# Centring x in its transposed layout instead of the weights, with row statistics on ScalarE and a reordered start and end

## The chip, the core and the metric

The kernel runs on one core of one Trainium2 chip. The metric is the device time of one execution in microseconds (us), median over several executions; less is better. A core has a matrix engine (PE; its weight loads are listed apart as PEld), VectorE (DVE), ScalarE (ACT), GpSimd (POOL) and SyncE (SP), which here only issues transfers. Each engine works through its own instructions strictly in order and waits on semaphores for the others. SBUF is the working memory, PSUM the memory that PE writes to.

## The reference

The input x is 4 sequences of 512 tokens with 512 features. Two blocks follow each other, each with a residual and a layer norm ahead of it:

```python
def _L0_attn_ref(x, W_q, W_kv, W_o):          # 16 heads of 32
    q  = (x @ W_q.T).reshape(B, S, H, hd)
    kv = (x @ W_kv.T).reshape(B, S, H, hd)
    qf  = _l2_normalize_complex(jnp.fft.fft(q, axis=-1))
    kvf = _l2_normalize_complex(jnp.fft.fft(kv, axis=-1))
    kvf = jnp.cumsum(kvf, axis=1)
    values_hat = jnp.fft.ifft(qf * kvf, axis=-1).real
    return values_hat.reshape(B, S, D) @ W_o.T
...
x = x + _L0_attn_ref(_layernorm(x), W_q, W_kv, W_o)
x = x + _L0_ffn_ref(_layernorm(x), gate_w, up_w, down_w, ...)   # silu(gate) * up, then down; 512 -> 1536 -> 512
```

The layer norm is (x - mean) / sqrt(var + 1e-5). The FFN's weights are rounded to float8_e4m3 first and its three products are scaled by vectors.

## The kernel before

**Setup.** The 2048 tokens are N = 16 chunks of 128 (four sequences of TC = 4 chunks). The Fourier transforms are 32x32 matrices, so they are multiplied into the weights at the start: `fold_in` turns W_kv and W_q (`raw[0]`, `raw[1]`) into `wkv` and `wq` by 16 matmuls of 128x128 each (two instructions per fp32 matmul, 32 in the profile), `fold_out` turns W_o into `wo`. A table tile `tab` holds the Fourier matrix (`fwd`, slot 0), the identity (slot 1), the inverse (slot 2) and a triangle of ones (slot 3). The transfer of slots 0 and 1 stands twice in the code (L91 and L110).

**How the mean is taken out.** q and kv are linear in x, so the mean over a token's 512 features can be removed by removing the mean over features from each row of the weights. That is `centered` (L149): for each of the four 128-row blocks of W_kv and W_q, DVE takes `bn_stats` and `bn_aggr`, then DVE (blocks 0 and 2 of W_kv) or ACT (all others, L158) subtracts. The reciprocal deviation of each token comes from `stats` (L259): `bn_stats`, `bn_aggr` and an addition of eps on DVE and a power on POOL (L266). It multiplies the spectra later.

**Rounds.** The loop over i = 0 .. 15 (L525) is a software pipeline, its order written out by hand (`tc.manual_schedule()`), so the order of the calls is the order on each engine. PE does per round `spectrum(i, 1)` (wkv, 8 matmul instructions), `v_transpose(i-2)` (four 128x128 transposes), `spectrum(i, 0)` (wq), `running(i-1)` (the cumulative sum of a chunk as a product with the triangle: `cum`) and `project(i-2)` (W_o: `po`). ACT squares the spectra (`squared`), DVE sums squares (`summed`), POOL takes the power -1/2 (`norms`, `rn`), DVE scales (`k_scaled`, `q_scaled`) and multiplies (`products`), POOL combines real and imaginary parts (`combined`). `carry` copies the last rows of a chunk's sum on ACT into `end` and sends the last one by DMA to the next chunk. `finish` adds the residual and stores the result to DRAM, `load_y` fetches it back for the FFN.

**FFN weights.** They come as 18 units of 128x1024, each rounded in four steps on DVE, ACT and POOL (`quant_abs`, `quant_step`, `quant_floor`, `quant_add`, `quant_sub`); `next_parts(n)` hands out the next n of these steps. What the rounds have not done is done inside the first FFN.

**FFN.** `ffn(b)` runs four times over m = 0 .. 11: two products `gu` (PSUM tag "b", two banks), `g` = silu on ACT (L456), `f` on DVE (L458), `fh` on ACT, `fl` on DVE, then the down product `pd`. In the last four steps m of one sequence the next one is prepared: `y_stats` (m = 8, 9), `y_norm` (m = 9, 10) and `y_transpose` (m = 10, 11; `pt_f`, `yh` on ACT, `yl` on DVE).

Work tiles come from rotating buffers: `end` and `cross` have one, most others two. PSUM has eight banks: four of tag "acc" (`pq`, `pw`, `pd`), two of "b" (`cum`, `po`, `gu`) and two of "tp" (`pt_v`, `pt_f`).

Of the kernel before, what the change touches and what calls it, by code (L numbers as in the profile page):

```python
# [30 lines left out]
def tile_fft_attention_then_fp8_ffn(  # L31
# [56 lines left out]


    tab = const.tile([P, 4, P], F32, name="tab")  # L90
    nc.sync.dma_start(tab[:, :2, :], tables[:, :2, :])  # L91
    fwd, ident, inv, tri = (tab[:, i, :] for i in range(4))

    xt, xTs = {}, {}
# [1 line left out]
    def load_xT(i):  # L96
        xTs[i] = work.tile([P, KC, P], F32, tag="xT", name=f"xT_{i}", bufs=3)
        nc.sync.dma_start(xTs[i], xT[i])

    def load_x(i):  # L100
        b, c = chunks[i]
        t = work.tile([P, D], F32, tag="x", name=f"x_{b}_{c}", bufs=6)
        nc.sync.dma_start(t, x[b, c * P : (c + 1) * P, :])
        xt[i] = t
# [2 lines left out]
        return big.tile([P, KC, D], dtype, tag="big", name=name)  # L107

    raw = []
    nc.sync.dma_start(tab[:, :2, :], tables[:, :2, :])  # L110
    for i, w in enumerate((w_kv, w_q, w_oT)):
        t = big_tile(f"raw{i}")
        for j in range(KC):
            nc.sync.dma_start(t[:, j, :], w[j * P : (j + 1) * P, :])
        raw.append(t)
        if i == 0:
            load_xT(0)
            nc.sync.dma_start(tab[:, 2:, :], tables[:, 2:, :])
        elif i == 1:
            load_x(0)  # L120
            load_xT(1)
            load_x(1)
    gus = const.tile([P, 2, MC], F32, name="gus")
    dsc = const.tile([P, D], F32, name="dsc")
    nc.scalar.dma_start(gus[:, 0, :], gate_scale)
    nc.scalar.dma_start(gus[:, 1, :], up_scale)
    nc.scalar.dma_start(dsc, down_scale.partition_broadcast(P))

    over = const.tile([P, 1], F32, name="over")
    nc.gpsimd.memset(over, -E4M3_OVERFLOW * DOWN * HUGE)  # L130

# [14 lines left out]
    wq = big_tile("wq")  # L146
    wo = big_tile("wo")

    def centered(r, j, on_act):  # L149

        t = r[:, j, :]
        st = work.tile([P, 6], F32, tag="st6", name=f"st_w{j}", bufs=3)
        nc.vector.bn_stats(st, t)
        mv = work.tile([P, 2], F32, tag="mv", name=f"mv_w{j}", bufs=8)
        nc.vector.bn_aggr(mv, st)
        if on_act:
            nc.vector.tensor_scalar(mv[:, 1:2], mv[:, 0:1], -1.0, None, ALU.mult)
            nc.scalar.activation(t, t, AF.Identity, bias=mv[:, 1:2])  # L158
        else:
            nc.vector.tensor_scalar(t, t, mv[:, 0:1], None, ALU.subtract)  # L160

    def fold_in(w, r):

        pw = [ps.tile([P, D], F32, tag="acc", name=f"pw{i}", bufs=4) for i in range(KC - 1)]
        pw.append(ps.tile([P, D], F32, tag="b", name=f"pw{KC - 1}"))
        for j in range(KC):
            for i in range(KC):
                nc.tensor.matmul(  # L168
                    pw[i][:, j * P : (j + 1) * P],
                    lhsT=r[:, j, i * P : (i + 1) * P],  # L170
                    rhs=fwd,
                    start=True,
                    stop=True,
                )
        for i in range(KC):
            (nc.scalar.copy, nc.vector.tensor_copy)[i % 2](w[:, i, :], pw[i])

    def fold_out(w, r):
        for j in range(KC):
            pw = ps.tile([P, D], F32, tag="acc", name="pw", bufs=4)  # L180
            nc.tensor.matmul(pw, lhsT=inv, rhs=r[:, j, :], start=True, stop=True)
            nc.scalar.copy(w[:, j, :], pw)


    U1 = 12
# [71 lines left out]


    def stats(src, name):  # L259
        st = work.tile([P, 6], F32, tag="st6", name=f"st_{name}", bufs=3)  # L260
        nc.vector.bn_stats(st, src)
        mv = work.tile([P, 2], F32, tag="mv", name=f"mv_{name}", bufs=8)
        nc.vector.bn_aggr(mv, st)
        rstd = work.tile([P, 1], F32, tag="rstd", name=f"rstd_{name}", bufs=8)
        nc.vector.tensor_scalar(rstd, mv[:, 1:2], EPS, None, ALU.add)  # L265
        nc.gpsimd.tensor_tensor(rstd, rstd, nhalf[:, 0:1], ALU.pow)  # L266
        return mv, rstd

    def normed(src, mv_rstd, name):
        mv, rstd = mv_rstd  # L270
        xn = work.tile([P, D], F32, tag="xn", name=f"xn_{name}")
        nc.vector.tensor_scalar(xn, src, mv[:, 0:1], rstd, ALU.subtract, ALU.mult)
        return xn

    def transpose(src, name):
# [5 lines left out]
    def heads(t):  # L281
        return t.rearrange("p (h f) -> p h f", f=HD)


    st_x, xns, pqs, sss, rns, qns, kns, carries, cums, qvs, qvTs, pos = (
        {} for _ in range(12)
    )

    def nm(i):
        return "%d_%d" % chunks[i]  # L290

    def x_stats(i):
        st_x[i] = stats(xt[i], f"a{nm(i)}")

    def spectrum(i, j):
        if j == 1:
# [9 lines left out]
    def squares(i, j):  # L306
        squared(i, j)
        summed(i, j)
# [82 lines left out]
        qvTs[i] = work.tile([P, KC, P], F32, tag="qvT", name=f"qvT_{nm(i)}")  # L391
        nc.scalar.copy(qvTs[i], pt)  # L392

    def project(i):
        po = ps.tile([P, D], F32, tag="b", name=f"po_{nm(i)}")
        qvT = qvTs.pop(i)
        for k in range(KC):
            nc.tensor.matmul(  # L398
                po, lhsT=qvT[:, k, :], rhs=wo[:, k, :], start=k == 0, stop=k == KC - 1
            )  # L400
        pos[i] = po
# [102 lines left out]
    def at(f, i, *more):  # L504
        if 0 <= i < N:
            f(i, *more)

    for j in range(KC):
        centered(raw[0], j, j % 2)
    fold_in(wkv, raw[0])  # L510
    x_stats(0)
    for j in range(KC):
        centered(raw[1], j, True)
    x_stats(1)
    nc.vector.tensor_copy(tri_r, tri)

    def attend(i):
        running(i)
        carry(i)
        products(i)  # L520
        combined(i)


    given = [4, 2, 2] + [3] * (N - 6) + [2, 2, 0]
    for i in range(N):  # L525
        at(spectrum, i, 1)
        if i == 0:
            load_unit(0)
            squares(0, 1)
            fold_in(wq, raw[1])  # L530
        if i == N - 6:
            load_y(0)
        at(load_xT, i + 2)
        if i > 2:
            k_scaled(i - 1)
        at(finish, i - 3)
        at(load_x, i + 2)
        if i > 2:
            k_low(i - 1)
        if i > 0:  # L540
            squared(i, 1)
        if i != 2:
            at(v_transpose, i - 2)
        if i > 0:
            next_parts(given[i] // 3, True)
        at(q_scaled, i - 1)
        if i > 0:
            summed(i, 1)
        at(norms, i, 1)
        if i == 0:  # L550
            fold_out(wo, raw[2])
        for c in pair(i - (N - 4)):
            y_stats(0, c)
        if i == 1:
            attend(0)
        at(spectrum, i, 0)
        if i == 0:
            quant_abs(0)
            next_parts(2, True)
        else:  # L560
            next_parts((given[i] + 1) // 3, True)
        if i == 2:
            v_transpose(0)
        if i > 1:
            running(i - 1)
        squared(i, 0)
        if i > 1:
            carry(i - 1)
        for c in pair(i - (N - 2)):
            y_transpose(0, c)  # L570
        for c in pair(i - (N - 3)):
            y_norm(0, c)
        if i > 1:
            products(i - 1)
            combined(i - 1)
        summed(i, 0)
        norms(i, 0)
        if i < 2:
            k_scaled(i)
            k_low(i)  # L580
        next_parts((given[i] + 2) // 3, True)
        at(x_stats, i + 2)
        at(project, i - 2)

# [7 lines left out]
    for b in range(B):  # L594

        def on_pe(m, part, b=b):
            if part == 0:
                if b == 0 and m < 2:
                    v_transpose(N - 2 + m)
                if b == 0 and m == 1:  # L600
                    finish(N - 2)
                return
            if b == 0 and m == 0:
                running(N - 1)
                products(N - 1)
                combined(N - 1)
                project(N - 2)
            if b + 1 < B and m >= MC - 2:
                for c in pair(m - (MC - 2)):
                    y_transpose(b + 1, c)  # L610

        def between(m, b=b):
            if b == 0 and m > 0:
                next_parts(1)

        def behind(m, b=b):
            if b == 0:
                if m == 1:
                    project(N - 1)
                    finish(N - 1)  # L620
                next_parts(2)
            if b + 1 < B:
                if m == 4:
                    load_y(b + 1)
                for c in pair(m - (MC - 3)):
                    y_norm(b + 1, c)
                for c in pair(m - (MC - 4)):
                    y_stats(b + 1, c)

        ffn(b, on_pe, between, behind)  # L630


# [60 lines left out]
```

## Time and profile before

| what | value |
|---|---|
| time, median of 3 executions | 492.27 us (490.43 to 492.43) |
| time of the profiled execution | 491.94 us |
| span of the profiled execution | 489.9 us |
| busy: PE, DVE, POOL, ACT | 470.2, 305.5, 180.2, 156.2 us |
| mean granted PE clock | 0.994 |

The span is what the profiler sees from the first to the last instruction; the time is 2.0 us more. A group's row gives busy time, the mean of one instruction in ns, and the idle time of the engine before these instructions with the engine, tile and line that ended it. The chain is followed back from the last instruction to whatever released each step. Matmuls are pipelined: the length of one is more than its distance to the next.

### The profile page before, as it was taken

To read this page: it belongs to the slowest core of one execution; us is meant where nothing else is said; L and a number is where in the kernel's file an instruction comes from. 1 tells how busy PE (TensorE), PEld (TensorE's weight loads), DVE (VectorE), ACT (ScalarE), POOL (GpSimd) and SP (SyncE) were. 2 spreads that over 40 slices of the span, in tenths; PEclk is the share of its full clock that TensorE was granted. 3 is DMA by queue.
4 is the path that set the end of the run, shared out by engine and by line. 5 is a ranking of instruction groups with operands and counts; after the bars stand their busy time and mean duration, and the time that the engine had idled before them with its cause. 6 is when DMAs were issued, how large, how long until landed. Compare 5 with 4: busy or idle time off the path is not lost.

```text
span 489.9 us, 4871 instructions
## 1 busy us (share of the span) xinstructions
PE 470.2 (96%) x1768; PEld 320.8 (65%) x1768; DVE 305.5 (62%) x499; ACT 156.2 (32%) x233; POOL 180.2 (37%) x124
## 2 busy tenths in 40 slices
PE   3999999999999999999998999999999999999995
PEld 3644444444444454568886888888888888888883
DVE  3757998889889997758788832237522246422225
ACT  2554433344433424323432322222222223222220
POOL 0226999888787975620212040001400000400002
PEclk9999999999999999999999899999999999999999
DMA  7912334115424200406000050000130000200002
GB/s 240 371 45 65 111 104 151 64 64 176 151 68 165 66 22 24 170 1 236 1 0 0 1 171 1 0 1 1 64 108 0 1 0 0 87 0 2 1 1 86
DMA packets 19080, 34.56 MB, mean 71 GB/s; under 512 B 2160, under 2 KB 2544, under 8 KB 19056
## 3 DMA queue, kind: packets, MB, share of 16 engines
q1 hardware_dynamic: 18240, 33.95, 20.3%
q10 hardware_dynamic: 816, 0.30, 0.2%
q8 instruction: 14, 0.23, 0.2%
q14 instruction: 10, 0.08, 0.1%
HBM read 25.83 MB, written 8.39 MB: 70 GB/s over the span
## 4 chain that ended last, share of the span: by engine, by line
PE 74%; DVE 16%; ACT 4%; issue 2%; POOL 1%; DMA 1%; ACTq 0%; SPq 0%; DVEq 0%
PE gu L445 34%; PE pd L483 18%; PE pq L301 11%; PE po L398 6%; PE pw L168 2%; DVE qa L237 2%; PE pt_f L278 1%; DVE ss L317 1%; DVE qm L233 1%; DVE kn L325 1%; ACT qa L226 1%; DVE qv L374 1%; DVE kl L347 1%; PE pt_v L278 1%; ACT kh L342 1%
## 5 line engine op out<-in xcount | busy, mean ns | idle before, releaser
L322 POOL TENSOR_TENSOR rn<-ss,nhalf 128x16 f32<-128x16 f32 x32 | 105.2, 3287 | 28.0 <-DVE ss L317 27.9
L458 DVE SCALAR_TENSOR_TENSOR f<-gu,gus,g 128x512 f32<-128x512 f32 x48 | 36.0, 751 | 107.2 <-PE gu L445 106.9
L483 PE MATMUL pd<-wd,fh 128*128 128x512 f32 x192 | 77.1, 401 | 0.0
L483 PE MATMUL pd<-wd,fl 128*128 128x512 f32 x192 | 76.6, 399 | 0.0
L445 PE MATMUL gu<-yh,wg 128*128 128x512 f32 x192 | 76.2, 397 | 0.4 <-DVE cross L376 0.4
L445 PE MATMUL gu<-yh,wu 128*128 128x512 f32 x192 | 74.9, 390 | 0.1
L445 PE MATMUL gu<-yl,wg 128*128 128x512 f32 x192 | 74.9, 390 | 0.0
L445 PE MATMUL gu<-yl,wu 128*128 128x512 f32 x192 | 74.8, 390 | 0.0
L456 ACT ACTIVATE g<-gu,gus 128x512 f32<-128x512 f32 x48 | 33.1, 689 | 97.4 <-PE gu L445 97.4
L463 ACT CAST fh<-f 128x512 fp32r<-128x512 f32 x48 | 29.8, 622 | 97.3 <-DVE f L458 97.3
L398 PE MATMUL po<-wo,qvT 128*128 128x512 f32 x128 | 57.7, 594 | 1.5 <-ACT qvT L392 0.8
L301 PE MATMUL pq<-wkv,xT 128*128 128x512 f32 x128 | 57.6, 593 | 0.0
L301 PE MATMUL pq<-wq,xT 128*128 128x512 f32 x128 | 57.6, 592 | 0.0
L496 POOL TENSOR_TENSOR o<-o,ys 128x512 f32<-128x512 f32 x14 | 17.7, 1293 | 90.7 <-issue 59.6
L266 POOL TENSOR_TENSOR rstd_f<-rstd_f,nhalf 128x1 f32<-128x1 f32 x16 | 8.8, 559 | 112.3 <-DVE rstd_f L265 112.3
L465 DVE TENSOR_TENSOR fl<-f,fh 128x512 fp32r<-128x512 f32 x48 | 33.2, 692 | 26.4 <-ACT fh L463 26.1
L301 PEld LDWEIGHTS pq<-wkv,xT 128*128 128x128 f32 x128 | 24.2, 190 | 30.3 <-issue 29.4
L445 PEld LDWEIGHTS gu<-yh,wg 128*128 128x128 f32 x192 | 36.2, 189 | 10.0 <-issue 1.7
L483 PEld LDWEIGHTS pd<-wd,fl 128*128 128x128 f32 x192 | 36.4, 190 | 8.6 <-DVE fl L465 0.2
L483 PEld LDWEIGHTS pd<-wd,fh 128*128 128x128 f32 x192 | 36.5, 190 | 8.2
L445 PEld LDWEIGHTS gu<-yl,wg 128*128 128x128 f32 x192 | 36.1, 188 | 8.2 <-issue 0.5
L398 PEld LDWEIGHTS po<-wo,qvT 128*128 128x128 f32 x128 | 23.9, 189 | 26.3 <-issue 23.0
(71 smaller groups left out, 584.8 us busy)
## 6 DMA issues: line engine op xcount, KB each, us to landing
xT<-in_xT SPq DMA_DIRECT2D x16, 256.0 KB, 2.8
x<-in_x SPq DMA_DIRECT2D x16, 256.0 KB, 2.8
y_all<-x SPq DMA_DIRECT2D x16, 256.0 KB, 2.0
ys<-y_all SPq DMA_DIRECT2D x4, 1024.0 KB, 5.7
out<-o SPq DMA_DIRECT2D x16, 256.0 KB, 2.0
rawf<-in_gate_w SPq DMA_DIRECT2D x3, 1024.0 KB, 5.5
rawf<-in_up_w SPq DMA_DIRECT2D x3, 1024.0 KB, 7.5
rawf<-in_down_w SPq DMA_DIRECT2D x3, 1024.0 KB, 6.1
```

The lines of the kernel that those rows point to most:

```text
L168: nc.tensor.matmul(pw[i][:, j * P : (j + 1) * P], lhsT=r[:, j, i * P : (i + 1) * P], rhs=fwd, start=True, stop=True,)
L237: nc.vector.scalar_tensor_tensor(a, m, ROUNDER / DOWN, w, ALU.mult, ALU.add)
L301: nc.tensor.matmul(pq, lhsT=xTs[i][:, k, :], rhs=w[:, k, :], start=k == 0, stop=k == KC - 1)
L322: nc.gpsimd.tensor_tensor(rns[i, j], sss.pop((i, j)), nhalf, ALU.pow)
L398: nc.tensor.matmul(po, lhsT=qvT[:, k, :], rhs=wo[:, k, :], start=k == 0, stop=k == KC - 1)
L445: nc.tensor.matmul(p, lhsT=w[:, k, m * P : (m + 1) * P], rhs=v[:, k, :], start=k == 0 and v is yh, stop=k == KC - 1 and v is yl,)
L456: nc.scalar.activation(g, pgu[0], AF.Silu, scale=gus[:, 0, m : m + 1])
L458: nc.vector.scalar_tensor_tensor(f, pgu[1], gus[:, 1, m : m + 1], g, ALU.mult, ALU.mult)
L463: nc.scalar.copy(fh, f)
L465: nc.vector.tensor_tensor(fl, f, fh.bitcast(F32), ALU.subtract)
L483: nc.tensor.matmul(pd[c], lhsT=v[:, c * P : (c + 1) * P], rhs=wd[:, n, :], start=n == 0 and v is fused[n][0], stop=n == MC - 1 and v is fu ...
L496: add.tensor_tensor(o, o, y[:, c, :], ALU.add)
```

## The change

x is centred instead of the weights. `centered` is gone. `stats` now runs on ACT: one pass sums a row (`accum_out`), a second small one makes minus the mean (`less`), a third sums the squared deviations, a fourth makes variance plus eps; POOL takes the power as before. This `stats` serves both the 16 chunks of x and the 16 of the FFN's input. Since x in its transposed layout (`xT`) has tokens along the free axis, the means are needed as a row: `x_row` spreads `less` over 128 columns and lets PE transpose it into a PSUM bank of tag "tp", and `x_center` adds that row to `xT` on DVE.

The order changes at the start, in rounds 0 and 1 (now written out), in the last three rounds, and in `behind`. Each table slot is sent once; x's first chunks are loaded earlier; the FFN's scale vectors are issued on SP's queue after the first round and no longer on ACT's at the start. `fold_in` is split into blocks, the first block of W_q going ahead of `spectrum(0, 1)`. The first two chunks of the first FFN input are transposed at the end of round N-2, its other two in round N-1; `project` of the last two chunks uses the banks of tag "tp".

```diff
-    nc.sync.dma_start(tab[:, :2, :], tables[:, :2, :])
+    nc.sync.dma_start(tab[:, 0, :], tables[:, 0, :])
...
-    nc.sync.dma_start(tab[:, :2, :], tables[:, :2, :])
     for i, w in enumerate((w_kv, w_q, w_oT)):
         t = big_tile(f"raw{i}")
         for j in range(KC):
             nc.sync.dma_start(t[:, j, :], w[j * P : (j + 1) * P, :])
+            if (i, j) == (0, 1):
+                load_x(0)
+                nc.sync.dma_start(tab[:, 1, :], tables[:, 1, :])
         raw.append(t)
         if i == 0:
             load_xT(0)
+        elif i == 1:
+            load_x(1)
+            load_xT(1)
             nc.sync.dma_start(tab[:, 2:, :], tables[:, 2:, :])
...
     def fold_out(w, r):
...
-            nc.scalar.copy(w[:, j, :], pw)
+            (nc.vector.tensor_copy, nc.scalar.copy)[j % 2](w[:, j, :], pw)
...
     def stats(src, name):
-        st = work.tile([P, 6], F32, tag="st6", name=f"st_{name}", bufs=3)
-        nc.vector.bn_stats(st, src)
-        mv = work.tile([P, 2], F32, tag="mv", name=f"mv_{name}", bufs=8)
-        nc.vector.bn_aggr(mv, st)
-        rstd = work.tile([P, 1], F32, tag="rstd", name=f"rstd_{name}", bufs=8)
-        nc.vector.tensor_scalar(rstd, mv[:, 1:2], EPS, None, ALU.add)
+        less = work.tile([P, 1], F32, tag="less", name=f"less_{name}", bufs=4)
+        rstd = work.tile([P, 1], F32, tag="dev", name=f"dev_{name}", bufs=6)
+        each = work.tile([P, D], F32, tag="end", name=f"each_{name}", bufs=1)
+        nc.scalar.activation(each, src, AF.Identity, accum_out=less)
+        nc.scalar.activation(less, less, AF.Copy, scale=-1.0 / D)
+        nc.scalar.activation(each, src, AF.Square, bias=less, accum_out=rstd)
+        nc.scalar.activation(rstd, rstd, AF.Identity, scale=1.0 / D, bias=eps)
         nc.gpsimd.tensor_tensor(rstd, rstd, nhalf[:, 0:1], ALU.pow)
...
+    def x_row(i):
+        rows[i] = ps.tile([P, KC, P], F32, tag="tp", name=f"mean_{nm(i)}")
+        nc.tensor.transpose(rows[i][:, 0, :], st_x[i][0].to_broadcast([P, P]), ident)
+
+    def x_center(i):
+        row = rows.pop(i)[:, 0:1, :].to_broadcast([P, KC, P])
+        nc.vector.tensor_tensor(xTs[i], xTs[i], row, ALU.add)
...
+    pkv = [ps.tile([P, D], F32, tag="acc", name=f"pkv{i}", bufs=4) for i in range(KC)]
     for j in range(KC):
-        centered(raw[0], j, j % 2)
-    fold_in(wkv, raw[0])
+        fold_in(pkv, raw[0], j)
     x_stats(0)
-    for j in range(KC):
-        centered(raw[1], j, True)
+    x_row(0)
+    folded(wkv, pkv)
+    x_center(0)
+    pw = ...
+    fold_in(pw, raw[1], 0)
     x_stats(1)
...
+    spectrum(0, 1)
+    squares(0, 1)
+    norms(0, 1)
+    for j in range(1, KC):
+        fold_in(pw, raw[1], j)
+    folded(wq, pw)
+    x_row(1)
+    x_center(1)
+    quant_abs(0)
+    k_scaled(0)
+    fold_out(wo, raw[2])
...
+    running(0)
+    carry(0)
+    x_stats(2)
...
+    spectrum(1, 1)
+    squares(1, 1)
+    norms(1, 1)
+    x_row(2)
+    x_center(2)
+    q_scaled(0)
+    products(0)
+    combined(0)
+    spectrum(1, 0)
...
-    for i in range(N):
+    for i in range(2, N):
...
         for c in pair(i - (N - 4)):
             y_stats(0, c)
-        if i == 1:
-            attend(0)
-        at(spectrum, i, 0)
+        spectrum(i, 0)
...
+        at(x_row, i + 1)
+        running(i - 1)
         squared(i, 0)
-        if i > 1:
-            carry(i - 1)
-        for c in pair(i - (N - 2)):
-            y_transpose(0, c)
-        for c in pair(i - (N - 3)):
-            y_norm(0, c)
+        carry(i - 1)
+        at(x_center, i + 1)
+        products(i - 1)
+        combined(i - 1)
+        if i == N - 1:
+            y_transpose(0, TC - 2)
+            y_transpose(0, TC - 1)
+        summed(i, 0)
+        norms(i, 0)
+        for c in pair(i - (N - 3)):
+            y_norm(0, c)
         next_parts((given[i] + 2) // 3, True)
         at(x_stats, i + 2)
-        at(project, i - 2)
+        project(i - 2)
+        if i == N - 2:
+            y_transpose(0, 0)
+            y_transpose(0, 1)
...
         def behind(m, b=b):
-            if b == 0:
-                if m == 1:
-                    project(N - 1)
-                    finish(N - 1)
-                next_parts(2)
+            if b == 0 and m == 1:
+                project(N - 1, "tp")
+                finish(N - 1)
             if b + 1 < B:
                 if m == 4:
                     load_y(b + 1)
                 for c in pair(m - (MC - 3)):
                     y_norm(b + 1, c)
+            if b == 0:
+                next_parts(2)
+            if b + 1 < B:
                 for c in pair(m - (MC - 4)):
                     y_stats(b + 1, c)
```

## The prediction

> **What bounds the kernel now.** First the page, for the engine that carries the span; then PE's waits, the order of time at the start, and the ends.
>
> ```profile
> span 489.9 us, 4871 instructions
> PE 470.2 (96%) x1768; PEld 320.8 (65%) x1768; DVE 305.5 (62%) x499; ACT 156.2 (32%) x233; POOL 180.2 (37%) x124
> PE 74%; DVE 16%; ACT 4%; issue 2%; POOL 1%; DMA 1%; ACTq 0%; SPq 0%; DVEq 0%
> ```
>
> PE is busy 470 of 490 us, so other engines matter only where PE waits. The view of PE's waits:
>
> ```profile
> PE pw L168 <- DVE raw L160: 7.8, 1, 7.8
> PE pt_f L278 <- DVE xn_f L272: 2.1, 1, 2.1
> PE pt_v L278 <- POOL qv L385: 1.4, 2, 1.0
> PE po L398 <- ACT qvT L392: 0.8, 1, 0.8
> PE po L398 <- DVE f L458: 0.7, 1, 0.7
> PE gu L445 <- DVE cross L376: 0.4, 1, 0.4
> ```
>
> Waits of 13.8 us in all (0.6 in smaller rows), 7.8 before the first matmul. The timeline shows what that start consists of:
>
> ```profile
> 0.72 0.37 SPq L91 DMA_DIRECT2D tab<-in_tables  x1
> 3.00 0.33 SPq L110 DMA_DIRECT2D tab<-in_tables  x1
> 3.38 2.02 SPq L114 DMA_DIRECT2D raw<-in_w_kv  x4
> 6.29 0.69 DVE L153 BATCH_NORM_STATS2 st_w<-raw 128x6 f32<-128x512 f32 x1 [6.29 <-DMA raw<-in_w_kv]
> 7.78 6.51 PE L168 MATMUL pw<-tab,raw 128*128 128x128 f32 x32 [7.78 <-DVE raw L160]
> 14.29 3.70 PE L301 MATMUL pq<-wkv,xT 128*128 128x512 f32 x8
> 17.98 4.18 PE L168 MATMUL pw<-tab,raw 128*128 128x128 f32 x32
> 22.16 3.70 PE L181 MATMUL pw<-raw,tab 128*128 128x512 f32 x8
> ```
>
> The second table transfer waits for the first, the weights stand behind it, then comes a mean. The same 32 matmuls take 6.51 us first and 4.18 us later: the early ones start 0.21 us apart, from 13.3 us on 0.11. The windows view around the one long late wait shows the clock falling there too:
>
> ```profile
> 265.90:269.30 3.40, 1.32 (x7) 0.79 (x5) 3.06 (x4) 0.29 (x1) 0.27 (x1) 1.00 0.00 0
> 269.30:272.70 3.40, 3.40 (x12) 3.03 (x13) 3.26 (x9) 0.36 (x1) 1.08 (x2) 0.51 0.00 0
> ```
>
> Columns: PE, PEld, DVE, ACT, POOL, clock, DMA. PE paused 2.1 us; in the next 3.4 us it had 0.51 of its clock. In rounds 3 to 13 PE has no gap: spectra start every 11.21 us. Between, from the groups split by shape:
>
> ```profile
> L158 ACT ACTIVATE raw<-raw,mv_w 128x512 f32<-128x512 f32 x6 | 4.3, 722 | 10.4 <-DVE mv_w L157 10.2 <-DMA rawf<-in_gate_w 0.3
> L463 ACT CAST fh<-f 128x512 fp32r<-128x512 f32 x48 | 29.8, 622 | 97.3 <-DVE f L458 97.3
> L134 ACT ACTIVATE table<-table 128x1 f32<-128x1 f32 x1 | 0.2, 202 | 0.0
> ```
>
> These price the new ACT work.
>
> **Start to fold_out.** With no second table, W_kv's first block is issued at 0.72 + 0.37 = 1.1 us. A 256 KB load takes 2.6 us at best here (shortest xT; first W_kv block 2.9), so it lands at 3.7 and PE starts at 3.75 instead of 7.78. Later blocks land 0.7 us apart and PE uses one in 1.7, so they don't hold it. The slow phase I take as the trace has it: 6.4 us from first to last, to 10.15. Rule against row: the Trainium skill (TensorE: Matmul & The Clock Gate, Part 1: The HAM clock gate) says half clock lasts until about 3.4 us of sustained work, in a window that runs freely; the trace had 5.6 us. By 3.4 us, 16 matmuls would be slow and 16 fast: 5.2 us, 1.2 better. I keep the trace; 1.2 goes into the range. The copies of wkv end 1.04 us after the last matmul (15.16 against 14.12), `x_center(0)` on DVE adds 0.69 (kl, 128x512): 11.9. PE meanwhile does the mean row and W_q's first block (1.0), and idles 0.55. Spectrum 3.69 from 11.95, the other three blocks 3.0, a row 0.15: `fold_out` starts at 18.8 instead of 22.16, -3.4. Bounds: -4.6 and -2.0 (late blocks: the third came at about 9.0, 4.5 us after its issue).
>
> **Rounds 0 and 1.** Walking the written order with the same durations: `carry(0)`'s DMA (row lands 1.8 us after issue) holds `x_stats(2)` on ACT, since `each` shares the single "end" buffer; behind it stand `qa_1` and sq1 of chunk 1; DVE waits for that sq1 ahead of `x_center(2)`; so spectrum(2,1) is 0.8 late. POOL then does rn0(0), rn1(1) (2.9 each) before qv: pt_v(0) 1.2 late. Before, the same stretch lost 1.5 us up to po(0) and 0.43 at pt_v(1). Net -0.2, between -1 and +1.5.
>
> **Mean rows.** Twelve more single transposes, chunks 4 to 15. pt_v's four take 0.435 us start to start in a stream (65.67 to 66.10), 0.11 each; with a change of operand I take 0.15: +1.8. Rule that speaks against the change: the same page (Part 4: PE-mode transpose) has about 275 ns each in a kernel, +3.3; the trace agrees with 273 ns as an instruction's length, but not as its share of PE's time. Ends +1.3 and +3.3. `x_center` (0.69) replaces 1.02 us of stats on DVE. It waits for the row, which PE makes just ahead of cum; behind it stand products, which had waited for `end` until 1 us after cum anyway, and spectrum(i+1,1) needs it 3.2 us later: nothing; uncovered it would be 0.69 a round. The row's bank, one of the two of tag "tp", is free again before the next pt_v.
>
> **Length s of one stats on ACT.** No row has an accumulating activation. Its four passes without that: 0.62 (no bias, as fh), 0.20, 0.72 (bias from a tile, as L158) and 0.30 (0.20 and the bias's 0.72 - 0.62), with three waits on the pass before of 0.04 (st_w to mv_w on DVE: 6.29 + 0.69 to 7.02): 1.96. With each accumulator read priced as the 128x1 row, 0.2, it is 2.36. I take 2.3. A gain below 1.96 is excluded: each pass must run. In the windows of rounds 11 to 13 ACT is busy 3.0 to 5.1 of 11.2 us, so one s a round is hidden. If it weren't, kh would be late first and PE would wait at `cum`.
>
> **Rounds 12 to 15.** Rounds 12 and 13 carry three s each: 6.9 + 4.8 of other work = 11.7 against 11.35. Counted from the start of round 12: ACT has kh(11), sq1(12), qvT(10) and the quant pass L226 done at 6.25, two y_stats last until 10.85, then come qa_10 (1.05) and sq0(12), done at 12.6, which a spectrum ending at 7.3 would allow at 8. DVE's ss0, quant_add and kn(12) follow at 15.2, kh(12), sq1(13) and qvT(11) at 17.1, two more y_stats until 21.7, sq0(13) and end(12) at 22.95. DVE takes products(12), ss0, two xn and the quant step behind it: 26.8; ACT's L226 waits for that step (27.95), `x_stats(15)` stands behind (30.25), kh(13) behind that (30.9), and kl ends at 31.6. PE could start cum(13) at 30.2 and is clear of it 1.6 late, waiting for qvT(12) too. Gone: pt_v's 1.0 and the 0.4 and 0.7 at the FFN's start (po no longer needs f's bank); a new 0.3 at pt_v(15). Net -0.2; ends -1.5 (s = 2.0) and +1.5 (2.55).
>
> **End of the first FFN.** Before, xn came after quant steps; now it goes first and 4.1 us of stats leave DVE. The 2.1 us go, and with them the half clock that followed: pt_f took 1.91 instead of 0.87, pd 2.62 instead of 1.87, 1.8. In exchange two y_stats at m = 8 and two at m = 9 stand ahead of g(9), g(10) on ACT. By g, f, fh, yh, yl, xn the second pt_f pair is just in time at s = 2.29; at 2.3 each of three hand-overs loses 0.05. Net -3.75, ends -3.9 and 0.
>
> **At nothing.** Scale vectors on SP: ahead of load_x(3), needed at 200 us; uncovered 0.7 us of transfers. x_0 and x_2, xT_2 are sent earlier, ahead of the first FFN weights: these landed at 21.1 (13.66 + 7.4) and now, with 128 KB more ahead and the stream 2 us sooner, at 19.4; ACT asks for them at 19.3 and has 0.5 us before kh(0) is late; uncovered, up to 1. Two wo copies on DVE beside fold_out. One quant step more in rounds, one less in FFN: DVE has room. The last o-add and store unchanged.
>
> **Sum** against the profiled 491.94: -3.4 - 0.2 + 1.8 - 0.2 - 3.75 = -5.75, so 486.2. The median of the runs, 492.27, is 0.33 above the profiled time.
>
> **Rivals.**
> 1. ACT becomes the limit, slower: if s is 2.8 (accumulator reads of 0.4). Slope: 7 us per us of s in rounds 12 to 14 (three s in each of two rounds, one after), 12 in the FFN (four s in series, three hand-overs). Against s = 2.3 that is +9.5: 495.7. Break-even near 2.6, slower by 0.5% from 2.75. For: ACT load 11.7 of 11.35 already. Against: the 0.2 row.
> 2. The start is bound by loads: W_kv and W_q blocks stretched as the third was, PE starting but waiting, stalls of rounds 0 and 1 doubled: head -0.5, sum about 489. With s = 2.45 beside it (+2.8) no change, 491.5.
> 3. The mean rows cost 0.3 to 0.4 each on PE: +2 to +3, 488.6. The change then does what it says and still gains.
> That centring x is not equivalent can be excluded: the projection is linear.
>
> **Numbers.** Forecast 0.60; rival 2 and mixtures near no change 0.20; rival 3 0.07; rival 1 0.13. What a measurement can tell from no change is about 0.5%, 2.5 us. Faster: 0.60 + 0.07 + 0.07 of rival 2 = 0.74; same 0.14; slower 0.12. Lowest: gate opening early (-1.2) and rows at 0.11 (-0.5), some bounds of rounds: 483.0. The upper end takes in the mixtures: 491.8.
>
> **What would show it.** Right: first L149 matmul near 3.8, fold_out near 19; PE waits at pt_f gone and clock 1.00 through the first FFN's end; rounds 11.36 us apart; four L247 to L250 instructions in 2.3 us. Wrong: accumulating passes over 0.9 us, PE waiting for kh or kl in rounds 13 and 14, for yl or xn at the hand-overs; first matmul after 5 us; rounds over 11.5 us.

## The result and the profile after

The changed kernel takes 487.0 us (median of 5, 486.5 to 487.3) against 492.27 (490.4 to 492.6): a ratio of 0.9905, 95% interval 0.9881 to 0.9929. The forecast was 486.2. The sum came out, but not its terms: the start and rounds 12 to 15 gained 3.1 us more than forecast, a loss of 3.6 us in the FFN was not in the forecast at all, and the two hid each other. The executions of the kernel before fall into two groups, near 490.1 and 492.1 us, and three of these five lie in the upper one; against the lower one the change gains about 3 us.

The page of the kernel after, its span, busy times and chain:

```profile
span 484.7 us, 5008 instructions
PE 471.6 (97%) x1784; PEld 318.6 (66%) x1784; DVE 281.6 (58%) x397; ACT 212.1 (44%) x417; POOL 184.4 (38%) x125
PE 82%; DMA 5%; DVE 4%; ACT 3%; POOL 3%; issue 2%; SPq 0%; ACTq 0%; DVEq 0%
```

DVE's busy time fell by 24 us and ACT's rose by 56, and DVE's share of the chain fell from 16% to 4%. PE, though it now waits less, is busy *longer* than before (470.2). PE's waits after:

```profile
PE pkv L149 <- DMA raw<-in_w_kv: 3.9, 1, 3.9
PE pt_v L263 <- POOL qv L378: 1.5, 2, 1.1
PE pw L149 <- DMA raw<-in_w_q: 0.7, 1, 0.7
PE pq L294 <- DVE xT L286: 0.4, 1, 0.4
PE cum L349 <- ACT g L449: 0.4, 1, 0.4
PE mean L282 <- ACT less L248: 0.3, 1, 0.3
PE cum L349 <- DVE kl L340: 0.2, 1, 0.2
```

They add up to 7.4 us instead of 13.8, but the span fell by 5.2 only. The start, from PE's timeline (start, length):

```profile
3.89 5.39 PE L149 MATMUL pkv<-tab,raw 128*128 128x128 f32 x32 [3.89 <-DMA raw<-in_w_kv]
10.08 1.16 PE L149 MATMUL pw<-tab,raw 128*128 128x128 f32 x8 [0.69 <-DMA raw<-in_w_q]
11.08 3.60 PE L294 MATMUL pq<-wkv,xT 128*128 128x512 f32 x8
17.30 3.88 PE L164 MATMUL pw<-raw,tab 128*128 128x512 f32 x8
```

The first matmul is 3.9 us earlier and `fold_out` 4.86 (17.30 against 22.16). At the end of the first FFN, where the kernel before paused and then lost its clock, the windows view shows PE busy throughout and the clock (last column but two) at 1.00:

```profile
257.23:263.62 6.39, 6.39 (x34) 5.25 (x32) 5.58 (x7) 5.38 (x16) 2.81 (x5) 1.00 0.01 3
263.62:270.10 6.48, 6.48 (x35) 5.34 (x34) 4.24 (x8) 2.72 (x5) 0.58 (x1) 1.00 0.00 0
```

Set against the trace before, by the starts of single matmuls:

| stretch on PE | forecast | measured |
|---|---|---|
| start to the other spectrum of round 3 (54.90 to 49.63) | -3.6 | -5.27 |
| from there to the first of round 12 (rows of chunks 4 to 12) | +1.35 | +1.60 |
| from there to the first `pd` (rows 13 to 15, rounds 12 to 15) | +0.25 | -1.20 |
| end of the first FFN | -3.75 | -3.85 |
| pace of the FFN everywhere else | 0 | +3.62 |
| to the last `pd` | -5.75 | -5.10 |

The last row but one is a term that the forecast did not have. One m of the FFN takes 5.593 us after, 5.520 before, in all four sequences, with the same 24 matmuls and no wait. The groups split by shape, over the undisturbed stretch from 290 to 470 us, before and then after:

```profile
L445 PE MATMUL gu<-yl,wu 128*128 128x512 f32 x128 | 49.9, 390 | 0.0
L445 PE MATMUL gu<-yh,wu 128*128 128x512 f32 x128 | 49.8, 389 | 0.0
L483 PE MATMUL pd<-wd,fh 128*128 128x512 f32 x129 | 51.4, 398 | 0.0
```

```profile
L438 PE MATMUL gu<-yh,wu 128*128 128x512 f32 x128 | 50.7, 396 | 0.0
L438 PE MATMUL gu<-yl,wu 128*128 128x512 f32 x128 | 50.5, 394 | 0.0
L476 PE MATMUL pd<-wd,fh 128*128 128x512 f32 x124 | 49.2, 397 | 0.0
```

Six nanoseconds an instruction: gu went from 389 to 395, to where pd was all along. From start to start, where no length is modelled, a gu followed the one before after 227.9 ns before and 233.5 ns after. That is what most of the experiments are about.

### The profile page after: what moved, and what is told of

Read it like the earlier page. It is cut to its first block, busy times and chain, and to the rows that moved or that the text cites. A ratio compares the mean times of both kernels' runs of the same rounds, so it can differ in the third digit from the quotient of the medians.

```text
span 484.7 us, 5008 instructions
## 1 busy us (share of the span) xinstructions
PE 471.6 (97%) x1784; PEld 318.6 (66%) x1784; DVE 281.6 (58%) x397; ACT 212.1 (44%) x417; POOL 184.4 (38%) x125
## 4 chain that ended last, share of the span: by engine, by line
PE 82%; DMA 5%; DVE 4%; ACT 3%; POOL 3%; issue 2%; SPq 0%; ACTq 0%; DVEq 0%
PE gu L438 36%; PE pd L476 18%; PE pq L294 15%; PE po L391 9%; POOL rn L315 2%; DMA row<-end 1%; DMA rawf<-in_gate_w 1%; DMA xT<-in_xT 1%; PE pt_v L263 1%; PE pt_f L263 1%; PE cum L349 1%; DMA raw<-in_w_kv 1%; ACT kh L335 1%; DVE kl L340 1%; ACT each L249 1%
## 5 line engine op out<-in xcount | busy, mean ns | idle before, releaser
L315 POOL TENSOR_TENSOR rn<-ss,nhalf 128x16 f32<-128x16 f32 x32 | 110.1, 3442 | 20.6 <-DVE ss L310 20.6
L438 PE MATMUL gu<-yh,wu 128*128 128x512 f32 x192 | 76.2, 397 | 0.0
L251 POOL TENSOR_TENSOR dev_f<-dev_f,nhalf 128x1 f32<-128x1 f32 x16 | 9.7, 611 | 108.4 <-ACT dev_f L250 108.3
L438 PEld LDWEIGHTS gu<-yl,wu 128*128 128x128 f32 x192 | 36.0, 188 | 8.6
L438 PEld LDWEIGHTS gu<-yh,wu 128*128 128x128 f32 x192 | 36.1, 188 | 8.6
```

The costliest lines, as they stand in the source:

```text
L315: nc.gpsimd.tensor_tensor(rns[i, j], sss.pop((i, j)), nhalf, ALU.pow)
L438: nc.tensor.matmul(p, lhsT=w[:, k, m * P : (m + 1) * P], rhs=v[:, k, :], start=k == 0 and v is yh, stop=k == KC - 1 and v is yl,)
```

## Experiments

**Where the tiles lie: three shifts of 32 bytes.** The change moved `gus` and `dsc` behind the weights and added `eps`, so yh and yl (pool "big") lie elsewhere relative to wg and wu. The first theory was that the two operands of a matmul want the same address modulo 64. All shifts use tiles that nothing reads:

```diff
+    const.tile([P, 1], F32, name="pad0")      # first run only
     wg = const.tile([P, KC, FF], F32R, name="wg")
...
     dsc = const.tile([P, D], F32, name="dsc")
+    const.tile([P, 1], F32, name="pad1")      # both runs
```

> The changed kernel with two unused 32-byte tiles, so that wg, wu, wd, yh, yl, fh and fl all start at 0 modulo 64 bytes. In the traces so far a gu or pd matmul starts 226 to 227 ns after the one before where its two operand tiles have the same address modulo 64 (gu before: 32 and 32), and about 233.6 ns (231, 232, 238 in turn) where they differ (gu after: 32 and 0; pd in both: 0 and 32). Theory, the pace follows from the two addresses: gu and pd both at 226 to 229 ns, the period of one m in the FFN 5.43 to 5.48 us instead of 5.593, total 480 to 481.5 us. Rival, the pace follows from what ACT, DVE and POOL do beside the matmuls, or differs from run to run: gu stays at 233, total 487.

> The changed kernel with one unused 32-byte tile behind dsc: the weights stay at 32 modulo 64, yh, yl, fh and fl move from 0 to 32. Theory of equal addresses: the same as with all at 0, gu and pd at 226 to 229 ns, 480 to 481.5 us. Rival, only tiles on a multiple of 64 are fast (then gu of the kernel before was fast for another reason): slower than with all at 0, gu and pd at 233 ns or more, 487 us or above. Rival, other engines set the pace: 487.

The third is the kernel before, with one such tile behind `wd`:

> The kernel before with one unused 32-byte tile behind wd: yh and yl move from 32 to 0 modulo 64, fh and fl from 0 to 32, the weights stay at 32. Theory of equal addresses: gu turns slow (226.5 to 233.6 ns) and pd turns fast (233.5 to 226.5), so the two change places; 16 matmuls gain about 5 ns each and 8 lose about 7 in one m, the period 5.52 becomes 5.54, the total rises by 1 us or less, 492 to 494. Rival, other engines set the pace: both stay as they were in the kernel before.

Measured: 485.48, 485.87 and 493.2 us. The first two gained 1.1 to 1.5 us instead of 6, so "modulo 64" fell. But the third, in which nothing but addresses moved, lost 0.35% (interval 0.18 to 0.53%), and its gu took on the pace of the changed kernel (290 to 470 us again):

```profile
L446 PE MATMUL gu<-yl,wu 128*128 128x512 f32 x125 | 49.4, 396 | 0.0
L446 PE MATMUL gu<-yh,wu 128*128 128x512 f32 x126 | 49.6, 394 | 0.0
```

In its trace one m takes 5.586 us instead of 5.520, which is 3.2 us over the 48 of them. The ratio shows less because nine of the sixteen executions of the kernel before beside it were of the upper group; the other seven have a median of 490.1. So the place of the tiles sets the pace, and the rule was wrong. What singled out gu in the kernel before was that yh and wg had equal addresses in many more low bits.

**All at multiples of 512.** Larger unused tiles in the same places, and one ahead of the work tiles:

```diff
+    work.tile([P, 112], F32, name="pad2", bufs=1)
...
+    const.tile([P, 56], F32, name="pad0")
     wg = const.tile([P, KC, FF], F32R, name="wg")
...
     dsc = const.tile([P, D], F32, name="dsc")
+    const.tile([P, 104], F32, name="pad1")
```

> The changed kernel with unused tiles so that the weights wg, wu, wd and the moving or stationary tiles yh, yl, fh, fl all start at multiples of 512 bytes. The runs with a shift of 32 bytes moved the pace but not by the rule modulo 64. Left is this: in the kernel before, wg and yh had the same address modulo 512 (352 and 352), and gu ran at 227.9 ns; in every other pairing seen (gu at a difference of 32, 96, 128; pd at 96, 128, 160, 192, all modulo 512 or 256) the mean lies between 230.8 and 234. Theory, equal addresses modulo 512 (the step from one 128-column slice of the weights to the next) are what is fast: gu and pd both 226.5 to 228 ns, the period of one m 5.43 to 5.47 us instead of 5.593, 6 to 8 us less than the changed kernel: 479 to 481 us. Rival, a property of the kernel before that has nothing to do with these differences: gu near 233, pd 231 to 233, 485 to 487 us.

480.03 us, 0.9778 of the kernel before (0.9752 to 0.9804), as the theory said. The same groups, all fast now:

```profile
L440 PE MATMUL gu<-yl,wu 128*128 128x512 f32 x131 | 51.0, 389 | 0.0
L440 PE MATMUL gu<-yh,wu 128*128 128x512 f32 x131 | 51.0, 389 | 0.0
L478 PE MATMUL pd<-wd,fh 128*128 128x512 f32 x131 | 51.3, 392 | 0.0
```

**Half of that, and the same for the kernel before.** Two more placements: yh and yl moved on by 256 bytes (`pad1` of 160 bytes, `pad2` of 704), and the kernel before with fh and fl moved so that they, too, agree with the weights.

> The changed kernel with weights, fh and fl at multiples of 512 bytes, and yh, yl at 256 modulo 512. If equality modulo 256 is enough, gu at 227 ns and the period of one m 5.44 us, 480 us; if the rule is modulo 512, gu at 231 to 234 and pd at 227, period 5.52 to 5.55, 484 to 485 us.

> The kernel before with one unused tile of 416 bytes ahead of the work tiles, so that fh and fl, like yh and yl already, have the same address as the weights modulo 512 (352). Nothing else of it is changed. Theory of equal addresses: gu stays at 227 ns, pd goes from 234 to 227, 7 ns times 8 matmuls times 48 = 2.7 us: 489.6 us where the half clock falls in, 487.7 where not. With this, both kernels have the same pace in the FFN, and what is left between this run and the changed kernel at multiples of 512 (480.0) is the change by itself: 8 to 9.5 us. Rival, the gain at multiples of 512 came from something else that the changed kernel alone has: pd stays at 234, 490.4 to 492.

480.06 us in a single execution, and 486.53 (ratio 0.9925, 0.9903 to 0.9947). The first answers its question by the pace in its trace: 256 is enough. The second missed on the size: the kernel before gained 3.9 us and not 2.7, because gu itself still had 1 ns to gain and the first gu behind pd had been slow as well (one m 5.520 to 5.440, times 48: 3.84). All placements together, with the addresses that the builds give ("operands apart" is the address of yh, yl, fh or fl minus that of its weights):

| kernel | gu: operands apart, mod 256 | gu, ns apart | pd: operands apart, mod 256 | pd, ns apart | one m, us |
|---|---|---|---|---|---|
| before | 0 | 227.9 | 96 | 234.0 | 5.520 |
| after | 96 | 233.5 | 160 | 233.2 | 5.593 |
| all at 0 mod 64 | 128 | 233.1 | 192 | 230.9 | 5.574 |
| all at 32 mod 64 | 128 | 232.9 | 192 | 230.8 | 5.573 |
| before, shifted by 32 | 32 | 232.9 | 128 | 232.4 | 5.586 |
| all at 0 mod 512 | 0 | 226.8 | 0 | 227.0 | 5.440 |
| yh, yl at 256 | 0 | 226.8 | 0 | 226.9 | 5.440 |
| before, all at 352 | 0 | 226.8 | 0 | 227.5 | 5.440 |

Every pairing at 0 runs at 227 to 228 ns, every other one tried at 231 to 234. It is the difference that counts and not a round address: the last row has all tiles at 352 modulo 512 and is as fast as all at 0. This also gives what the change is worth with the pace out of the way: 486.53 to 480.03, 6.5 us. That is less than the 8 to 9.5 expected, since the kernel before gained more by its placement than I had priced and only one of its six executions was of the upper group.

**The end of the first FFN: the order, or the move to ACT?** First the order alone, in the kernel before:

```diff
-            if b == 0:
-                if m == 1:
-                    project(N - 1)
-                    finish(N - 1)
-                next_parts(2)
+            if b == 0 and m == 1:
+                project(N - 1)
+                finish(N - 1)
             if b + 1 < B:
                 if m == 4:
                     load_y(b + 1)
                 for c in pair(m - (MC - 3)):
                     y_norm(b + 1, c)
+            if b == 0:
+                next_parts(2)
+            if b + 1 < B:
                 for c in pair(m - (MC - 4)):
                     y_stats(b + 1, c)
```

> The kernel before with only the order at the end of the first FFN changed: xn (y_norm) goes ahead of the quant steps, the statistics behind them, and stay on VectorE. Theory, the step of the forecast (the wait at pt_f of 2.1 us and the half clock behind it of 1.8 us come from the order alone): the wait goes, the clock stays at 1.00 through the end of the first FFN, 3.7 to 3.9 us less, 488.4 us. Rival, VectorE stays late because it still has 4.1 us of statistics there: a wait of about 1 us remains, half clock or not, 490 to 491.5.

489.98 us, ratio 0.997 (0.9952 to 0.9987): nearer the rival. The first pair of `pt_f` no longer waits, the second does, since DVE is still behind there. From its timeline:

```profile
271.43 0.50 PE L445 MATMUL gu<-yh,wu 128*128 128x512 f32 x1 [0.26 <-DVE f L458]
274.90 1.09 PE L278 MATMUL pt_f<-tab,xn_f 128*128 128x128 f32 x8 [1.36 <-DVE xn_f L272]
```

The clock stays up, but the m with the second pair takes 10.39 us where its like in the later sequences takes 8.26: the pause of 2.1 us has only moved by one pair. Against the seven executions of the kernel before in the lower group (median 490.1) the order alone gains nothing that is clear of noise.

Then the reverse: the changed kernel with only the statistics of y back on DVE as `bn_stats`.

> The changed kernel with the statistics of y (16 of them) back on VectorE as bn_stats, those of x left on ScalarE. Theory, the end of the first FFN needs both the order and the move (with the order alone PE still waited 1.4 us at the second pair of pt_f and 0.5 behind it): a wait of 1.4 to 2 us returns at the second pair, and at the FFN's start; rounds 12 to 14 lose less than 0.8 at cum(13), since ScalarE is freer and VectorE fuller; total 488 to 489.5. Rival, the order alone is worth it in this kernel, and statistics on ScalarE cost time in rounds 12 to 14: 486 to 486.5, faster than the changed kernel.

487.13 us, the same as the changed kernel:

```profile
270.32 1.08 PE L263 MATMUL pt_f<-tab,xn_f 128*128 128x128 f32 x8 [0.44 <-DVE xn_f L257]
```

The wait at the second pair is 0.44, not 1.4 to 2; that stretch loses 0.63 us and rounds 12 to 15 gain 0.38. So my theory fell: in the changed kernel the move of y's statistics is nearly even. What else removed the pause was not isolated. One part can be seen on DVE: in the first of these two runs it still does a quant step between the last statistics and `fl`, and in the second, with one step more done in the rounds, it has none there:

```profile
271.29 1.21 DVE L241 SCALAR_TENSOR_TENSOR wd<-qm,qa 128x1024 fp32r<-128x1024 f32 x1
```

The slower pace of PE in the changed kernel, 0.07 us for each m, also leaves DVE more time. How much each is worth stays open.

**The start.** The changed kernel with two table slots sent twice again:

```diff
-    nc.sync.dma_start(tab[:, 0, :], tables[:, 0, :])
+    nc.sync.dma_start(tab[:, :2, :], tables[:, :2, :])
...
+    nc.sync.dma_start(tab[:, :2, :], tables[:, :2, :])
     for i, w in enumerate((w_kv, w_q, w_oT)):
...
-                nc.sync.dma_start(tab[:, 1, :], tables[:, 1, :])
```

> The changed kernel with the first two tables sent twice ahead of the weights again, as in the kernel before, and nothing else of it undone. Theory of the forecast (of the 4 us by which the first matmul came earlier, the second table's wait was 2.3 and the mean of W_kv's blocks 1.5): the first matmul at 6.1 to 6.4 us instead of 3.89, fold_out and the end 2 to 2.5 us later, 489 to 489.5 us. Rival, the start is bound by later loads or by the clock gate: the first matmul moves by 2.3 us, the end by less than 1, 487.5 us.

488.77 us (1.8 more than the changed kernel), with the first matmul at 6.36:

```profile
6.36 5.30 PE L149 MATMUL pkv<-tab,raw 128*128 128x128 f32 x32 [6.36 <-DMA raw<-in_w_kv]
13.20 3.70 PE L294 MATMUL pq<-wkv,xT 128*128 128x512 f32 x8 [0.53 <-DVE xT L286]
```

2.5 us at the first matmul, 2.1 at the first spectrum, 2.2 at the last `pd`: in this trace what is lost there is not won back later. The other 1.4 us up to the 7.78 of the kernel before were the weights' mean.

**A mean row, made twice.**

```diff
         nc.tensor.transpose(rows[i][:, 0, :], st_x[i][0].to_broadcast([P, P]), ident)
+        nc.tensor.transpose(rows[i][:, 1, :], st_x[i][0].to_broadcast([P, P]), ident)
```

The page that this expectation speaks of is the forecast's second one, the Trainium skill (TensorE: Matmul & The Clock Gate, Part 4: PE-mode transpose).

> The changed kernel with each mean row made twice (a second transpose of the same operand into the next 128 columns of the same bank, which nothing reads): 16 more single transposes on PE. By the share that pt_v's four have in a stream, 0.11 us each: 1.8 us more, 488.8. By the forecast's 0.15: 2.4, 489.4. By the page's 0.275 (the length of the instruction): 4.4, 491.4. Rounds 4 to 11, where PE has no gap, tell it best: 11.32 us apart now, then 11.43, 11.47 or 11.6.

487.12 us, 0.1 more. The rounds say 0.11 each: spectra 11.43 us apart instead of 11.32 (57.55, 68.97, 80.40), although the groups show the length of 273 ns:

```profile
L282 PE MATMUL mean<-tab,less 128*128 128x128 f32 x16 | 4.4, 276 | 0.3 <-ACT less L248 0.3
L283 PE MATMUL mean<-tab,less 128*128 128x128 f32 x16 | 4.4, 273 | 0.0
```

The total hardly moved because waits took it up: the one of 0.36 at `pt_v` in round 7 went, and rounds 12 to 15 with three more transposes were 0.24 shorter than without. What one stretch loses another gives back as long as a wait on another engine stands between; my expectation of the total forgot that.

**A better version.** With tiles at multiples of 512, zeros for PE until data lands:

```diff
+    warm = const.tile([P, P], F32, name="warm")
+    nc.vector.memset(warm, 0.0)
+    pwarm = ps.tile([P, D], F32, tag="b", name="pwarm")
+    for n in range(12):
+        nc.tensor.matmul(pwarm[:, :P], lhsT=warm, rhs=warm, start=True, stop=True)
```

> The changed kernel at multiples of 512, with twelve 128x128 matmuls of zeros on PE from about 1 us on, before any data has landed; nothing reads their result. In ten profiled runs the clock came up 3.1 to 5.9 us after the first matmul. Theory: it now comes up at 4.3 to 7 us instead of 7.2 to 9.8, and at most 12 of the 32 first real matmuls are slow instead of 14 to 27; the first spectrum starts at 11.0 us in every run, bound by W_q's first block (10.04 in the changed kernel), where the runs so far had 11.0 to 12.1; 479.0 to 479.8 us. Rival, matmuls of zeros do not count for the clock, or delay the first real ones: 480 or above.

479.54 us; the runs (478.7 to 479.8) overlap those without (479.6 to 480.4), so a gain is not shown. Zeros do count for the clock (6.57 us, 5.5 after the first), but twelve lasted too long:

```profile
1.04 5.49 PE L99 MATMUL pwarm<-warm 128*128 128x128 f32 x24 [1.04 <-DVE warm L96]
6.32 3.86 PE L157 MATMUL pkv<-tab,raw 128*128 128x128 f32 x32
```

Then six, together with a buffer of its own for the scratch output that held `x_stats(2)`:

```diff
-    for n in range(12):
+    for n in range(6):
...
-    def stats(src, name):
+    def stats(src, name, tag="end", bufs=1):
...
-        each = work.tile([P, D], F32, tag="end", name=f"each_{name}", bufs=1)
+        each = work.tile([P, D], F32, tag=tag, name=f"each_{name}", bufs=bufs)
...
-        st_x[i] = stats(xt[i], nm(i))
+        st_x[i] = stats(xt[i], nm(i), *(("xn", 2) if i < N - 4 else ()))
```

> The run with zeros ahead of the data, at multiples of 512, with two edits: six matmuls of zeros instead of twelve (each was two PE instructions of 0.213 us, so that twelve lasted until 6.31 us and held the first real one back from 4.0), and the scratch output of x's statistics for chunks 0 to 11 in the two idle xn buffers, so that x_stats(2) no longer waits for carry(0)'s row transfer on the shared end buffer. Theory: the first real matmul at 3.9 us again, the clock up between 4.3 and 7 us, the first spectrum at 11.0 to 11.3 (11.7 with twelve, 12.1 with none in that draw), bound by W_q's first block; the forecast's step of rounds 0 and 1 says that spectrum(2,1)'s wait of 0.5 goes, and pt_v(0)'s 1.1 shrinks as far as POOL's order allows: 478.3 to 479.2 us. Rival, both are absorbed by the wait at pt_v(0), which the two rn on POOL set: 479.5, as with twelve.

477.68 us (477.4 to 478.7), 0.9743 of the kernel before (0.9718 to 0.9768), the fastest here and below the 478.3 to 479.2 expected. In its trace the zeros gained nothing, since W_kv's third block came late; the buffer did:

```profile
4.02 2.36 PE L157 MATMUL pkv<-tab,raw 128*128 128x128 f32 x16
8.14 2.05 PE L157 MATMUL pkv<-tab,raw 128*128 128x128 f32 x16 [1.75 <-DMA raw<-in_w_kv]
32.61 3.60 PE L302 MATMUL pq<-wkv,xT 128*128 128x512 f32 x8
37.34 0.66 PE L271 MATMUL pt_v<-tab,qv 128*128 128x128 f32 x4 [1.13 <-POOL qv L386]
```

The run with twelve zeros had:

```profile
33.64 3.70 PE L302 MATMUL pq<-wkv,xT 128*128 128x512 f32 x8 [0.39 <-DVE xT L294]
38.48 0.66 PE L271 MATMUL pt_v<-tab,qv 128*128 128x128 f32 x4 [1.14 <-POOL qv L386]
```

Both first spectra stand at 11.7 us, yet spectrum(2,1) is at 32.61 instead of 33.64 and `pt_v(0)` at 37.34 instead of 38.48, with its wait of 1.1 unchanged: all of POOL's work ahead of it moved up too, so the rival fell.

## Why the prediction was right, and where not

**Start to fold_out: right in kind, too small (-3.4, measured -4.86).** First matmul 3.89 (3.75 forecast), no weights' mean. The largest mis-sized term is the clock. I took the 6.4 us of the trace for the 32 instructions instead of the rule's 5.2; they took 5.1. Neither is "right": the clock came up 3.1 to 5.9 us after the first matmul in twelve profiled runs of this case (before 5.6, after 3.3, at multiples of 512 5.8), and the trace was one draw near the top. Of these 1.3 us, 0.14 went back at the first matmul and 0.3 at W_q's first block: PE waited 0.7 for it, and `spectrum(0, 1)` came at 11.08, while `x_center(0)` was done at 10.76. The other 0.6 is lengths that I took for distances: the spectrum, three blocks of W_q and a row took 6.22 us from start to start, not 6.84. Of the terms put at nothing, the first gate weights came at 20.58 and not at 19.4, and ACT stood 2.8 us for them, but PE shows no wait for `kh(0)`.

**Rounds 0 and 1: right.** -0.2 forecast, -0.4 found between `fold_out` and round 3. `x_stats(2)` behind `carry(0)`'s transfer and `pt_v(0)`'s wait of 1.1 are in the trace as written, and the last run took the first away for a gain of 1.0.

**Mean rows: right, 0.11 rather than 0.15.** The length of about 275 ns that the Trainium skill gives for a transpose inside a kernel (TensorE: Matmul & The Clock Gate, Part 4: PE-mode transpose) is in the groups above (276 and 273 ns), but the doubled rows show that it is not the price. Of the +1.60 to round 12, 1.0 is nine rows and most of the rest waits of POOL at `pt_v`.

**Length s of one stats: 2.12 to 2.20 us, not 2.3.** The groups of ACT, split by form:

```profile
L247 ACT ACTIVATE each<-x 128x512 f32<-128x512 f32 x16 | 10.0, 625 | 15.1 <-DMA row<-end 8.7 <-DMA x<-in_x 6.3
L247 ACT ACTIVATION_READ_ACCUMULATOR each<-x 128x1 f32 x16 | 3.0, 189 | 0.0
L248 ACT ACTIVATE less<-less 128x1 f32<-128x1 f32 x16 | 3.3, 203 | 0.5
L249 ACT ACTIVATE each<-x,less 128x512 f32<-128x512 f32 x16 | 11.6, 724 | 0.6
L250 ACT ACTIVATE dev<-dev,eps 128x1 f32<-128x1 f32 x16 | 4.7, 296 | 0.5
```

A second accumulator read of 188 ns follows L249. Every duration was within 0.02 of the forecast's, the accumulator reads too; they sum to 2.23 and overlap by about 0.1, where I had counted 0.1 of waits on top. Rival 1 (s = 2.8) is far off.

**Rounds 12 to 15: mis-sized (-0.2 forecast, about -1.5 without their three rows).** With the shorter s, cum(13) was 0.85 late (from `spectrum(14, 0)` to `pt_f` 8.29 us, 7.44 for the same work a round earlier) and not 1.6, the 0.3 at `pt_v(15)` did not come, and 0.4 remained at the FFN's start.

**End of the first FFN: right for the profiled execution (-3.85).** But half of that term is not in every execution. The kernel before falls into two groups of times, 489.4 to 490.6 with a mean clock of 0.998 or more and 491.5 to 493.1 with 0.994 to 0.997; the 1.8 us of half clock belong to the second: one window of 3.41 us at half clock takes 0.0035 off a mean over 490 us, which is about the distance between the groups. Of 51 further executions of that kernel, taken beside the experiments, 32 lie in the first group (median 490.1) and 19 in the second (492.1), so the change gained 3.1 us against the one and 5.1 against the other. The trace of the kernel before is of the second; here it stands against those of two variants with the same pause (before, shifted by 32, and before, all at 352), in windows counted off from the moment when the clock first came up:

```profile
265.93:269.34 3.41, 1.33 (x7) 0.82 (x6) 3.10 (x4) 0.26 (x1) 0.24 (x1) 1.00 0.00 0
269.34:272.75 3.41, 3.41 (x13) 3.02 (x14) 3.27 (x9) 0.41 (x1) 1.08 (x2) 0.50 0.00 0
```

```profile
266.54:269.96 3.42, 1.85 (x8) 1.15 (x7) 2.66 (x3) 0.69 (x1) 0.69 (x1) 1.00 0.00 0
269.96:273.37 3.41, 3.02 (x17) 2.61 (x18) 3.27 (x10) 0.00 (x0) 1.08 (x2) 1.00 0.00 0
```

```profile
263.88:267.29 3.41, 1.68 (x8) 1.06 (x6) 2.57 (x3) 0.65 (x1) 0.77 (x1) 1.00 0.00 0
267.29:270.71 3.42, 2.94 (x17) 2.59 (x18) 3.28 (x10) 0.00 (x0) 1.08 (x2) 1.00 0.00 0
```

Pauses of 2.1, 2.0 and 2.2 us; in the first PE was busy for 1.33 of a window's 3.41 us and the next window ran at half clock, with 1.85 and 1.68 it did not. So in these traces not the pause's length but its place in the window decided. A sum made against a profiled execution should have said that this term comes and goes.

**Missing: the pace of the FFN (+3.62).** The forecast compared instructions, waits and clocks, and took the cost of an unchanged matmul as unchanged. The diff did show the cause: three lines of allocation that moved. Without this term the parts would have come to -8.7 us against the profiled execution, 483.2, at the very edge of the range; the middle was met because the start and rounds 12 to 15 gave 3.1 us more than forecast and the pace took 3.6. That the number came so near is luck, and so is part of the base: the profiled execution was of the upper group. What the trace bears out is the path and the sign of each named term. Rivals 2 and 3 find no support: loads stretched (a wait of 0.7 at W_q), but the start still gained more than forecast, and rows are cheap.

## What to carry to other kernels

Compare the start-to-start time of the matmuls that the change does not touch; a few ns on a thousand of them outweigh a stall that one can see, and a moved allocation is enough to cause them. Before pricing a stall's aftermath or a warm-up from one trace, look at several executions: what depends on the phase of a window is a range, not a number. And take an instruction's price on a busy engine from the distance between neighbours, not from its length.

## What the runs showed of the hardware

- An fp32r matmul of 128x128 by 128x512 followed the one before after 227 to 228 ns where its two SBUF operands had equal start addresses modulo 256, after 231 to 234 ns at differences of 32, 96, 128, 160 and 192. 64 and 224 were not tried, and why it is so stays open. Over 1152 such matmuls it is 5.593 against 5.440 us for each m, 7 us in all.
- The clock moves in steps of one window of 3413 ns: the half-clock stretch of the kernel before lasted 3413 ns, and the stretches at full clock are multiples of it. In all fourteen traces it came up at the end of the first window in which PE was busy for 3.1 us or more (2.5 us and less left it down) and was lost at the end of one with 1.34 us or less (1.66 us and more kept it), so the delay after the first matmul depends on where the window falls. The Trainium skill (TensorE: Matmul & The Clock Gate, Part 1: The HAM clock gate) has this free-running window, and the runs agree; its spread of 0.5 us for the time until the clock comes up is too narrow here (3.1 to 5.9 us).
- Matmuls of zeros raise the clock like any others (5.5 and 3.7 us after the first, in the two runs that had them).
- In the changed kernel each ACT pass with `accum_out` is followed by a second instruction, ACTIVATION_READ_ACCUMULATOR, of 0.19 us.
